# A two-layer graph network: indexed stores without addition, and the residual added by VectorE from PSUM

## The chip, the cores and the metric

The kernel runs on one core of a Trainium2 chip. The metric is the device time of one execution in microseconds; the median of several runs is given. PE is TensorE (matrix products), DVE is VectorE, ACT is ScalarE, POOL is GpSimd, SP is the engine that only issues DMAs here. Each engine takes its instructions in a fixed order, and an instruction that waits holds up all behind it on its engine.

## The reference

There are 16 graphs of 1024 nodes with 64 features each, and a weighted adjacency matrix of 1024 x 1024 for each. Cut to what matters:

```python
# layer 0
h = maximum(layernorm(x), 0)
deg = clip(sum(adj, axis=2, keepdims=True), 1.0, None)
x = x + matmul(adj / deg, h)

# layer 1
h = maximum(layernorm(x), 0)
adj_d = dilate(adj, mask)     # self loops set; of a node with over 10 neighbours every
                              # skip-th one is removed, in both directions
agg = weighted sum of the 0.25, 0.5 and 0.75 quantiles (weights 0.25, 0.5, 0.25) of
      h over the neighbours in adj_d, feature by feature
y = relu((h + agg) @ W1 + b1) @ W2 + b2
x = x + y * mask
```

`W1` is 64 x 128 and `W2` is 128 x 64. The last line is the one that the change is about: each node's result is its residual `x` after layer 0 plus its masked sum.

## The kernel before, in words

**A planner writes the order.** The kernel is built from Python generators ("streams"). Each stream yields the engine that it needs next and a time before which it shouldn't start. `Plan` (from L231) keeps an estimated clock for each engine and for every tile the time at which it is ready, always runs the stream that can start first, and records the instructions. Their order on every engine is therefore settled when the program is built, from estimated costs. Since every instruction passes through one helper, most of them carry line 225 in the profile; one goes by tile names. Two margins occur in what follows: a stream asks to start `SLACK` = 2 us, or `LOOSE` = 7 us, after the estimated time at which its input is ready. `room(name, n)` is the estimated time at which the oldest of n buffers is free again. Any indirect DMA on POOL is estimated at 1.27 us (L292).

**Layer 0**, graph by graph (streams `loads`, `beginnings`, `signs`, `listing`, `transposes`, `products`, `channels`, `endings`). SP loads the adjacency matrix in eight tiles `at` of 128 x 1024, with five buffers. ACT takes their signs, DVE makes of each row a list of neighbours (32 candidates, `rec`), PE transposes them and multiplies by the normalised features. The result x1 (the residual) is written into a tile `row` (L565), which for each node holds, in this order: 64 normalised features and two index columns (width W = 66), the record of 34 columns (the list, the node's number and its mask) and the residual of 64. `channels` (L700) normalises x1, stores the residual of the whole graph to `out` (L708), and the features to a table `tab` in DRAM (L709). `endings` (L714) gives every node a place by the length of its list, and POOL stores the features and the record (100 columns) to that place of a sorted table `srt` with eight indirect DMAs for each graph (L775). Four graphs share one `srt`; there are four such groups.

**Layer 1** works on 128 nodes of like list length at once. `group` (L1016) loads the records of a sorted table and makes ten `Job`s, of one to six tiles of 128 nodes, with lists of 15 neighbours down to 1. A job (L808) loads the nodes' own rows (`S`, L821) by SP, gathers the neighbours' rows from `tab` with one indirect DMA on POOL for each tile and neighbour (`places`), and sorts them on DVE with a network of minimum and maximum operations. The quantiles are products with weights (`prod`). `long_lists` (L1134) does the same for the longest lists, 20 to 88 neighbours (`lplaces`), with one tile of 128 nodes for each.

**The layers' end** is `layers` (L964). For up to four tiles at a time: PE sums and transposes the terms into `pt`, ACT evacuates it to `ot`, PE multiplies by `W1` into PSUM, ACT applies bias and relu (`hid`), PE multiplies by `W2` and adds the bias `b2`: for each tile there is one product of 128 x 64, and one of a row of ones with `b2_sb`. ACT then multiplies by the mask into `y` (L1003 to L1007), and POOL adds `y` to the nodes' rows of `out`, with an indirect DMA that adds to what stands there (L1012). The four buffers of `y` are freed by the store.

```python
for i, t in enumerate(ts):
    nc.tensor.matmul(pv[:, i, :], hid[:, i * P:(i + 1) * P], w2_sb, start=True, stop=False)
    nc.tensor.matmul(pv[:, i, :], ones_f[:1, :], b2_sb, start=False, stop=True)
yield "ACT", lambda: at(py) + SLACK
for i, t in enumerate(ts):
    nc.scalar.activation(y[:, t, :], pv[:, i, :], AF.Copy, scale=self.mask[:, t:t + 1])
```

Stores to one table have no order among themselves, since they go to different rows; `scatter` (L786) declares that, and puts a small memset of the tile `turn` between two stores to the same table that follow one another directly. All this is `list_path` (L364). A second path, `dense_path`, is only taken when a list overflows, and doesn't run on these inputs.

Of the kernel before, what the change touches and what calls it, by code (L numbers as in the profile page):

```python
# [9 lines left out]
F32 = mybir.dt.float32  # L10
# [4 lines left out]
AF = mybir.ActivationFunctionType  # L15
OP = mybir.AluOpType
AX = mybir.AxisListType

P = 128
# [8 lines left out]
GB = 4  # L28
# [184 lines left out]
SLACK = 2.0  # L213
LOOSE = 7.0
# [16 lines left out]
class Plan:  # L231
# [132 lines left out]
def list_path(ctx, tc, x, adj, nodemask, w1, b1, w2, b2, out, go):  # L364
    nc = tc.nc
    B, N, C = x.shape
    H = w1.shape[1]
    CO = w2.shape[1]
    NT = N // P
    HALF = 512  # L370
    BPH = HALF // P
    NG = B // GB
    TS = N + 1
    W = C + 2
    PW = W // 2
    REC = 8 * NSEG + 2
    R0 = W
    X1 = RW = R0 + REC
    NTAU = N // SUB
    NF = NG + NG + len(LONG)  # L380

# [58 lines left out]
    nc.sync.dma_start(w2_sb, w2)  # L440
    b1_sb = consts.tile([H, 1], F32, name="b1_sb")
    nc.sync.dma_start(b1_sb, b1.rearrange("(h o) -> h o", o=1))
    b2_sb = consts.tile([1, CO], F32, name="b2_sb")
    nc.sync.dma_start(b2_sb, b2.rearrange("(o c) -> o c", o=1))
    taus = consts.tile([P, len(QUANTILES)], F32, name="taus")
    for k, (tau, wt) in enumerate(QUANTILES):
        nc.vector.memset(taus[:, k:k + 1], tau)
# [24 lines left out]
    scatters = []  # L472
    sorts = [[] for _ in range(NG)]
    plan = Plan(nc)
    nc = plan.nc
# [79 lines left out]
    def beginnings(pool, now):  # L555

        for b, st in enumerate(batch):
            now[0] = b
            yield "DVE", lambda: max(known(st, "xt", "mrow"), room("h0", 3), room("row", 4))
            mrow_f = new(tiny, [NT, P], F32, "mrow_f", 2)  # L560
            nc.vector.tensor_copy(mrow_f, st["mrow"])

            h0 = new(pool, [P, NT, C + 1], F32, "h0", 3, users=2)
            nc.vector.memset(h0[:, :, C:], 1.0)
            row = st["row"] = new(pool, [P, NT, X1 + C], F32, "row", 4, users=1)  # L565
            nc.vector.memset(row[:, :, C:W], -1.0)
            yield from normed(h0[:, :, :C], st["xt"])
            st["h0"] = h0
            yield "PE", lambda: max(at(mrow_f), room("ps_small", 3))
            pm = new(ps_s, [P, HALF], F32, "ps_small", 3, users=1)  # L570
            nc.tensor.transpose(pm[:, :NT], mrow_f, ident[:NT, :NT])
            yield "ACT", lambda: at(pm)
            nc.scalar.copy(row[:, :, RW - 1], pm[:, :NT])
            nc.scalar.copy(row[:, :, RW - 2], row_f)
            free(pm)
# [79 lines left out]
    def products(pool, now):  # L655


        for b, st in enumerate(batch):
            now[0] = b
            for hf in range(2):  # L660
                yield "PE", lambda: INF if st["copied"][hf] < 2 * BPH else max(
                    at(st["att"][hf]), known(st, "h0"), room("ps_small", 3)
                )
                po = new(ps_s, [P, HALF], F32, "ps_small", 3, users=1)
                for q in range(NT):
                    if q and q % 2 == 0:
# [12 lines left out]
                pb = new(ps_s, [P, HALF], F32, "ps_small", 3, users=1)  # L679
                sums = pb[:, :BPH * (C + 1)].rearrange("p (k c) -> p k c", c=C + 1)  # L680
                for k in range(BPH):
                    nc.tensor.transpose(
                        sums[:, k, :], msg[:, k * P:(k + 1) * P], ident[:C + 1, :C + 1]
                    )
                yield "DVE", lambda: at(pb) + SLACK
                x1 = st["row"][:, hf * BPH:(hf + 1) * BPH, X1:]
                deg = new(tiny, [P, BPH], F32, "deg", 2)
                nc.vector.tensor_scalar(deg, sums[:, :, C], 1.0, None, op0=OP.max)
                nc.vector.reciprocal(deg, deg)
                nc.vector.tensor_tensor(  # L690
                    x1, sums[:, :, :C], deg.unsqueeze(2).to_broadcast([P, BPH, C]), OP.mult
                )
                nc.vector.tensor_tensor(
                    x1, x1, st["xt"][:, hf * BPH:(hf + 1) * BPH, :], OP.add
                )
                free(pb)
                st["residual"] += 1
            free(st["xt"])

    def channels(pool, now):  # L700

        for b, st in enumerate(batch):
            now[0] = b
            row = lambda: st["row"]
            yield "DVE", lambda: known(st, "row") if st["residual"] == 2 else INF
            yield from normed(row()[:, :, :C], row()[:, :, X1:])

            nc.sync.dma_start(out[b].rearrange("(t p) c -> p t c", p=P), row()[:, :, X1:])  # L708
            nc.sync.dma_start(  # L709
                tab[b * TS:b * TS + N, :].rearrange("(t p) w -> p t w", p=P), row()[:, :, :W]  # L710
            )
            st["normed"] = True

    def endings(pool, now):  # L714

        first = lambda rank: rank - 3000
        for b, st in enumerate(batch):
# [54 lines left out]
            nc.vector.scalar_tensor_tensor(to, low, float(1 - GB), pos, op0=OP.mult, op1=OP.add)  # L772
            for t in range(NT):
                yield "POOL", lambda: max(at(to), at(row)) + LOOSE if "normed" in st else INF, first
                scatter(srt[g], row[:, t, :RW], to[:, t:t + 1], sorts[g])  # L775
            free(row)
            progress["batches"] = b + 1

# [4 lines left out]
            in_offset=bass.IndirectOffsetOnAxis(ap=idx, axis=0),  # L783
        )

    def scatter(dst, src, idx, others, op=OP.bypass):  # L786
        if plan.last is others:
            nc.gpsimd.memset(turn, 0.0)
        ins = nc.gpsimd.indirect_dma_start(
            out=dst, out_offset=bass.IndirectOffsetOnAxis(ap=idx, axis=0),  # L790
            in_=src, in_offset=None, compute_op=op,
        )

        for other in others:
            tc.declare_no_dep(ins.ins, other, reason="rows of their own")
        others.append(ins.ins)
        plan.last = others

    class Job:
# [8 lines left out]
        def run(self):  # L808
# [9 lines left out]
            progress["ahead"] += T * (n - 1)  # L818
            if short:
                mine = self.S  # L820
                self.S = new(pool, [P, T, W], F32, "S", 4, users=1)  # L821
                nc.sync.dma_start(self.S, mine)
            for t in range(T):
                for k in range(n - 1):
                    if t or k:
# [138 lines left out]
        def layers(self, terms, sources):  # L964

            T, R = self.T, terms[0][0].shape[1]
            yield "PE", lambda: max(at(*sources) + LOOSE, room("y", 4), room("pt", 2))
            y = new(mlp, [P, T, CO], F32, "y", 4, users=1)
            for t0 in range(0, T, 4):
                ts = range(t0, min(t0 + 4, T))  # L970
                M = len(ts) * P
# [23 lines left out]
                yield "PE", lambda: max(at(hid) + SLACK, room("ps_small", 3))  # L995
                py = new(ps_s, [P, HALF], F32, "ps_small", 3, users=1)
                pv = py[:, :len(ts) * CO].rearrange("p (t c) -> p t c", c=CO)
                for i, t in enumerate(ts):
                    nc.tensor.matmul(
                        pv[:, i, :], hid[:, i * P:(i + 1) * P], w2_sb, start=True, stop=False  # L1000
                    )
                    nc.tensor.matmul(pv[:, i, :], ones_f[:1, :], b2_sb, start=False, stop=True)
                yield "ACT", lambda: at(py) + SLACK  # L1003
                for i, t in enumerate(ts):
                    nc.scalar.activation(
                        y[:, t, :], pv[:, i, :], AF.Copy, scale=self.mask[:, t:t + 1]
                    )  # L1007
                free(py)
            for t in range(T):
                yield "POOL", lambda: at(y) + LOOSE  # L1010
                rows = out_rows[:min(self.g + 1, NG) * GB * N, :]
                scatter(rows, y[:, t, :], self.nodes_i[:, t:t + 1], scatters, OP.add)  # L1012
            free(y)
            progress["jobs"][self.g] += 1

    def group(g):  # L1016
# [107 lines left out]
        for i, ts in enumerate(classes):  # L1124
            n, T = CAPS[ts[0]] + 1, len(ts)
            sl = slice(ts[0], ts[-1] + 1)
            job = Job(
                gat, n, T, keys[:, sl, :n - 1], idx[:, sl, :], node[:, sl], mask[:, sl],
                nodes_i[:, sl], table, tiles[:, sl, :W], g,
            )  # L1130
            plan.add(job.run(), 100 * g + i)
        progress["groups"] = g + 1
# [393 lines left out]
```

## Time and profile before

| | |
|---|---|
| median of 3 runs | 1586.0 us (1583.88 to 1586.02) |
| the profiled execution's own time | 1823.34 us, of which the profile's span is 1821.4 |
| indirect DMAs of POOL | 660 gathers of rows from `tab`, 128 stores to `srt`, 128 stores to `out` |
| `y` on ACT | 128 instructions, 0.313 us each in the median |
| bias products on PE | 256 passes |
| moved by DMA | 124.89 MB, 69 GB/s over the span |
| mean granted clock of TensorE | 0.653 of full speed |

The profiled execution is longer than the timed ones, since recording costs time. Durations and differences below are therefore read inside the profile and compared with its own length. In the page, a group of instructions is named by what it writes and reads (`out<-in`), with its count, busy time and mean duration, and after the second bar the time that its engine stood idle just before it, with what ended that idle time. A releaser called "issue" is none that the profile shows. PE makes two passes for one product in fp32, and each is counted.

### The profile page before, as it was taken

How to read it: one execution, taken by the hardware profiler on the slowest of the kernel's cores; microseconds unless marked ns; L12 is line 12 of the kernel's file. 1: busy time of each engine (PE TensorE's matmuls, PEld its weight loads, DVE VectorE, ACT ScalarE, POOL GpSimd, SP SyncE). 2: the span in 40 equal slices, each digit the busy share in tenths (PEclk: the TensorE clock that was granted, in tenths of full speed). 3: DMA queues.
4: the chain of work that ended last, by engine and by line, in shares of the span. 5: the costliest groups of instructions: out<-in, count | busy, mean ns of one | idle time of the engine just before them, and what ended most of it. 6: DMA issues, size and time to landing. Idle time of an engine off the chain costs nothing. (4 is left out here: it accounts for less than half of the span.)

```text
span 1821.4 us, 15210 instructions
## 1 busy us (share of the span) xinstructions
PE 825.6 (45%) x3336; PEld 533.0 (29%) x3336; DVE 1240.1 (68%) x4046; ACT 609.3 (33%) x1874; POOL 1050.8 (58%) x1144
## 2 busy tenths in 40 slices
PE   5767822365686572563685000110031366253364
PEld 3333411233444341232354000100021245242343
DVE  7865858475788486678642889339497678896622
ACT  8877653245655464444442000000010111010011
POOL 0112263636467655555758766567656788575757
PEclk8978855675798675775885555555555567555656
DMA  5544741233444353353222211101111112111112
GB/s 170 163 133 122 199 125 31 48 101 81 121 134 112 58 134 91 90 138 73 56 48 49 43 43 34 23 17 22 28 24 28 18 26 20 23 30 23 24 18 17
DMA packets 147941, 124.89 MB, mean 69 GB/s; under 512 B 117715, under 2 KB 117843, under 8 KB 147843
## 3 DMA queue, kind: packets, MB, share of 16 engines
q1 hardware_dynamic: 102818, 86.58, 16.8%
q0 software_dynamic: 45024, 37.28, 12.2%
q14 instruction: 71, 0.57, 0.1%
q8 instruction: 28, 0.46, 0.1%
HBM read 104.51 MB, written 19.28 MB: 68 GB/s over the span
## 5 line engine op out<-in xcount | busy, mean ns | idle before, releaser
L225 POOL DMA_INDIRECT places<-tab,idx x496 | 495.0, 998 | 165.1 <-issue 140.2
L225 PE MATMUL pt<-ident,prod 128*128 128x128 f32 (+1 forms) x736 | 161.8, 384 | 569.4 <-DVE prod L225 294.5
L225 POOL DMA_INDIRECT out_dram<-y,nodes_i x124 | 208.0, 1678 | 186.8 <-ACT y L225 127.4
L225 PEld LDWEIGHTS pt<-ident,prod 128*128 128x128 f32 (+1 forms) x736 | 134.2, 267 | 605.3 <-issue 389.7
L225 POOL DMA_INDIRECT srt<-row,to x128 | 129.4, 1011 | 259.0 <-ACT row L225 223.5
L225 PE MATMUL pt<-ident,at 128*128 128x128 f32 x1024 | 190.0, 334 | 179.6 <-ACT att L225 72.1
L225 PE MATMUL ps_small<-att,h 128*65 128x512 f32 x512 | 259.0, 652 | 17.7 <-ACT h L225 10.3
L225 PEld LDWEIGHTS pt<-ident,at 128*128 128x128 f32 x1024 | 143.5, 171 | 236.5 <-ACT att L225 97.7
L225 POOL DMA_INDIRECT lplaces<-tab,lidx x163 | 171.0, 1049 | 49.7 <-issue 49.1
L225 ACT COPY att<-pt 128x512 f32<-128x512 f32 x256 | 142.9, 583 | 155.7 <-remote 84.2
L225 DVE MAX8 rec<-sg 128x8 f16<-128x256 f16 x512 | 180.1, 414 | 9.5 <-remote 5.2
L225 ACT ACTIVATE wu<-wu 128x39 f32<-128x39 f32 (+9 forms) x40 | 9.4, 234 | 431.7 <-DVE wu L225 168.8
L225 ACT ACTIVATE sg<-at 128x1024 f16<-128x1024 f32 x128 | 134.9, 1055 | 31.7 <-DMA at<-in_adj_dram 15.3
L225 DVE TENSOR_TENSOR sg<-sg,keyed 128x1024 f16<-128x1024 f16 x128 | 87.4, 683 | 65.5 <-issue 33.4
L225 PEld LDWEIGHTS ps_small<-att,h 128*65 128x65 f32 x512 | 75.4, 153 | 149.4 <-issue 126.5
L225 ACT COPY ot<-pt 128x128 f32<-128x128 f32 (+3 forms) x56 | 22.4, 400 | 246.7 <-remote 128.2
L225 PE MATMUL ps_small<-ot,w_sb 128*128 128x128 f32 (+3 forms) x112 | 55.9, 593 | 104.7 <-ACT ot L225 72.6
L225 PE MATMUL ps_small<-w_sb,hid 128*128 128x64 f32 x256 | 72.5, 376 | 52.6 <-ACT hid L225 25.1
L225 DVE TENSOR_TENSOR other<-places,other 128x64 f32<-128x64 f32 (+6 forms) x204 | 69.5, 341 | 35.6 <-remote 16.3
L225 PEld LDWEIGHTS ps_small<-w_sb,hid 128*128 128x128 f32 x256 | 53.6, 258 | 80.5 <-ACT hid L225 40.3
L225 DVE TENSOR_TENSOR rem<-places,recs 128x30 f32<-128x30 f32 (+9 forms) x40 | 7.3, 182 | 101.7 <-DMA places<-tab,idx 90.0
L225 POOL MEMSET turn<- 128x1 f32 x204 | 76.2, 373 | 0.1
(206 smaller groups left out, 1712.2 us busy)
## 6 DMA issues: line engine op xcount, KB each, us to landing
at<-in_adj_dram SPq DMA_DIRECT2D x128, 512.0 KB
places<-tab,idx POOLq DMA_INDIRECT x496
tab<-row SPq DMA_DIRECT2D x16, 264.0 KB
xt<-in_x_dram SPq DMA_DIRECT2D x16, 256.0 KB
out_dram<-row SPq DMA_DIRECT2D x16, 256.0 KB
lplaces<-tab,lidx POOLq DMA_INDIRECT x163
recs<-srt SPq DMA_DIRECT2D x4, 544.0 KB
srt<-row,to POOLq DMA_INDIRECT x128
```

What stands on the lines that cost most here:

```text
L225: ins = getattr(self._engine, op)(*args, **kwargs)
```

## The change

The residual no longer goes to `out` early. It becomes part of the rows that POOL sorts (164 columns in place of 100), and is added in the last step of layer 1.

- The tile `row` is laid out anew: features and index columns, residual, record. The whole row is stored to `srt`.
- The 16 stores of the residual to `out` by SP go.
- `S` is loaded with 64 columns in place of 66. A job with short lists keeps a reference to the residual's columns, and loads them into the tile `y` at the head of `layers`, by SP. A long list has them in its `S` already.
- `b2_sb` holds the bias four times, and one product of the row of ones with up to 256 columns takes the place of up to four; it comes first in the group.
- The last sum is formed by VectorE: PSUM times mask plus residual, in place into `y`. It is planned `LOOSE` after the product, where ACT's was planned `SLACK` after it. `y` has five buffers, not four.
- The indirect store to `out` is a plain one, and names all rows of `out`.

```diff
-    R0 = W
-    X1 = RW = R0 + REC
+    X1 = W
+    R0 = X1 + C
+    RW = R0 + REC
...
-    b2_sb = consts.tile([1, CO], F32, name="b2_sb")
-    nc.sync.dma_start(b2_sb, b2.rearrange("(o c) -> o c", o=1))
+    b2_sb = consts.tile([1, 4 * CO], F32, name="b2_sb")
+    for k in range(4):
+        nc.sync.dma_start(b2_sb[:, k * CO:(k + 1) * CO], b2.rearrange("(o c) -> o c", o=1))
...
-            yield from normed(row()[:, :, :C], row()[:, :, X1:])
-
-            nc.sync.dma_start(out[b].rearrange("(t p) c -> p t c", p=P), row()[:, :, X1:])
+            yield from normed(row()[:, :, :C], row()[:, :, X1:R0])
...
-                scatter(srt[g], row[:, t, :RW], to[:, t:t + 1], sorts[g])
+                scatter(srt[g], row[:, t, :], to[:, t:t + 1], sorts[g])
...
-                self.S = new(pool, [P, T, W], F32, "S", 4, users=1)
-                nc.sync.dma_start(self.S, mine)
+                self.S = new(pool, [P, T, C], F32, "S", 4, users=1)
+                nc.sync.dma_start(self.S, mine[:, :, :C])
+                self.residual = mine[:, :, X1:R0]
...
-            yield "PE", lambda: max(at(*sources) + LOOSE, room("y", 4), room("pt", 2))
-            y = new(mlp, [P, T, CO], F32, "y", 4, users=1)
+            yield "PE", lambda: max(at(*sources) + LOOSE, room("y", 5), room("pt", 2))
+            y = new(mlp, [P, T, CO], F32, "y", 5, users=1)
+            x1 = y
+            if self.short:
+                nc.sync.dma_start(x1, self.residual)
+            else:
+                x1 = self.S[:, :, X1:R0]
...
+                nc.tensor.matmul(
+                    py[:, :len(ts) * CO], ones_f[:1, :], b2_sb[:, :len(ts) * CO],
+                    start=True, stop=False,
+                )
                 for i, t in enumerate(ts):
                     nc.tensor.matmul(
-                        pv[:, i, :], hid[:, i * P:(i + 1) * P], w2_sb, start=True, stop=False
+                        pv[:, i, :], hid[:, i * P:(i + 1) * P], w2_sb, start=False,
+                        stop=(i == len(ts) - 1),
                     )
-                    nc.tensor.matmul(pv[:, i, :], ones_f[:1, :], b2_sb, start=False, stop=True)
-                yield "ACT", lambda: at(py) + SLACK
+                yield "DVE", lambda: at(py) + LOOSE
                 for i, t in enumerate(ts):
-                    nc.scalar.activation(
-                        y[:, t, :], pv[:, i, :], AF.Copy, scale=self.mask[:, t:t + 1]
+                    nc.vector.scalar_tensor_tensor(
+                        y[:, t, :], pv[:, i, :], self.mask[:, t:t + 1], x1[:, t, :],
+                        op0=OP.mult, op1=OP.add,
                     )
                 free(py)
+
             for t in range(T):
                 yield "POOL", lambda: at(y) + LOOSE
-                rows = out_rows[:min(self.g + 1, NG) * GB * N, :]
-                scatter(rows, y[:, t, :], self.nodes_i[:, t:t + 1], scatters, OP.add)
+                scatter(out_rows, y[:, t, :], self.nodes_i[:, t:t + 1], scatters)
```

Since the planner's estimates and waits change, it writes another order for all engines, from the first microseconds on.

More of the change, by code (lines that the diff above doesn't have):

```diff
@@ L564, in beginnings @@
             nc.vector.memset(h0[:, :, C:], 1.0)
-            row = st["row"] = new(pool, [P, NT, X1 + C], F32, "row", 4, users=1)
+            row = st["row"] = new(pool, [P, NT, RW], F32, "row", 4, users=1)
             nc.vector.memset(row[:, :, C:W], -1.0)
@@ L685, in products @@
                 yield "DVE", lambda: at(pb) + SLACK
-                x1 = st["row"][:, hf * BPH:(hf + 1) * BPH, X1:]
+                x1 = st["row"][:, hf * BPH:(hf + 1) * BPH, X1:R0]
                 deg = new(tiny, [P, BPH], F32, "deg", 2)
@@ L784, in gather, with scatter @@
         )
-    def scatter(dst, src, idx, others, op=OP.bypass):
+    def scatter(dst, src, idx, others):
         if plan.last is others:
@@ L790, in scatter @@
             out=dst, out_offset=bass.IndirectOffsetOnAxis(ap=idx, axis=0),
-            in_=src, in_offset=None, compute_op=op,
+            in_=src, in_offset=None,
         )
@@ L1128, in group @@
                 gat, n, T, keys[:, sl, :n - 1], idx[:, sl, :], node[:, sl], mask[:, sl],
-                nodes_i[:, sl], table, tiles[:, sl, :W], g,
+                nodes_i[:, sl], table, tiles[:, sl, :R0], g,
             )
```

## The prediction

> **What bounds the kernel now.** I read the page first: busy time by engine and the forty slices.
>
> ```profile
> span 1821.4 us, 15210 instructions
> ...
> PE 825.6 (45%) x3336; PEld 533.0 (29%) x3336; DVE 1240.1 (68%) x4046; ACT 609.3 (33%) x1874; POOL 1050.8 (58%) x1144
> ...
> PE   5767822365686572563685000110031366253364
> ...
> DVE  7865858475788486678642889339497678896622
> ...
> POOL 0112263636467655555758766567656788575757
> ```
>
> No engine is full over the span, and there are two stages. In the first 22 slices PE, ACT and DVE work together (layer 0); later PE and ACT are nearly empty and only DVE and POOL stay busy. The tile view of `srt` puts the last sorting store at 988.4 us, so I cut at 990 and asked for busy time by window:
>
> ```profile
> core 0: us, PE busy (x) PEld busy (x) DVE busy (x) ACT busy (x) POOL busy (x), PEclk, DMA share, GB/s
> 0.00:990.00 990.00, 590.65 (x2345) 348.17 (x2346) 674.76 (x2252) 545.58 (x1670) 488.47 (x600) 0.73 0.40 104
> ```
>
> Then the groups of POOL alone from 990 to 1822 (count, busy, mean; after the second bar the idle time ahead of them and what ended it):
>
> ```profile
> L225 POOL DMA_INDIRECT places<-tab,idx x243 | 247.0, 1016 | 75.2 <-issue 67.1 <-DMA places<-tab,idx 4.6 <-DMA tab<-drop,didx 1.4
> L225 POOL DMA_INDIRECT lplaces<-tab,lidx x163 | 171.0, 1049 | 49.7 <-issue 49.1 <-DMA lplaces<-tab,lidx 0.6
> L225 POOL DMA_INDIRECT out_dram<-y,nodes_i x73 | 125.2, 1715 | 111.2 <-ACT y L225 77.2 <-ACT prod L225 21.1 <-issue 12.0
> ...
> L225 POOL DMA_INDIRECT out_dram<-y,lnodes_i x4 | 6.5, 1626 | 5.3 <-ACT wu L225 4.4 <-issue 0.9
> ```
>
> The "issue" gaps of 0.3 us stand between any two indirect DMAs and belong to them. Gathers so cost 247.0 + 75.2 + 171.0 + 49.7 = 543 us. The 77 result stores take about 1.89 us from start to start (below), 145 us. Waits for `y` and what is booked with them are 77.2 + 21.1 + 4.4 = 103 us, the rest (adjacency gathers and their waits) about 28. Together 819 of 832 us: the second stage is POOL's queue, with 103 us of holes in which it stands at a store whose sum isn't there.
>
> The timeline of POOL shows what one store costs, accumulating first, plain second:
>
> ```profile
> 1758.43 1.58 POOL L225 DMA_INDIRECT out_dram<-y,nodes_i  x1 [0.19 <-issue]
> 1759.44 0.68 POOL L225 MEMSET turn<- 128x1 f32 x1
> 1760.32 1.57 POOL L225 DMA_INDIRECT out_dram<-y,nodes_i  x1 [0.19 <-issue]
> ```
>
> ```profile
> 246.64 0.98 POOL L225 DMA_INDIRECT srt<-row,to  x1 [0.19 <-ACT row L225]
> 247.62 0.11 POOL L225 MEMSET turn<- 128x1 f32 x1
> 247.93 0.97 POOL L225 DMA_INDIRECT srt<-row,to  x1 [0.19 <-issue]
> ```
>
> Start to start, 1760.32 - 1758.43 = 1.89 us against 247.93 - 246.64 = 1.29. At the end of the program seventeen stores follow one another at this rate, to a last start at 1812.35, and nothing comes after them. In the first stage POOL waits instead: 205.9 of its idle us before 926 end on `row` from ACT.
>
> **What the Trainium skill says.** "DMA: Bandwidth & Descriptors", SWDGE vs HWDGE vs iDMA: an accumulating DMA can be issued by GpSimd only, and GpSimd cores compute the descriptors of indirect DMAs. The trace agrees: all 128 are POOL's, at a median of 1.58 us against 0.97 for a plain store; the page has no price for the accumulation. "Perfetto Trace Analysis", DMA Instruction — SWDGE (GPSIMD): the shown duration ends with the last descriptor written, not with the data. So 1.58 and 0.97 are POOL's own time, and it is POOL that the change relieves. "SBUF — State Buffer", Who interferes with whom: a VectorE instruction with at most one SBUF tensor outside the two-port modes doesn't contend with GpSimd; the new sum reads PSUM and one SBUF tensor. No run here shows that instruction.
>
> **The change part by part.** Sums are of the profiled execution: its time is 1823.34 us, the span 1821.4 and 1.9 around it. The median of the runs is 1586.0, 0.870 of it; which rows recording lengthens isn't visible, so I scale differences by 0.870.
>
> *Plain stores.* 1.89 - 1.28 (between 1.27 and 1.29 for `srt`) = 0.61 us each, 128 x 0.61 = 78 us of POOL. The order of the two programs says where: after the last sorting store there are 77 result stores and 406 gathers now, 83 and 399 after. Second stage: stores 145 to 83 x 1.28 = 106, -39; gathers 543 to 399 x 543/406 = 534, -9. Together -48 us. The first stage holds 45 stores (51 now) and 7 gathers more. It saves POOL 51 x 1.89 - 45 x 1.28 - 7 x 1.34 = 29 us, but waits for rows there take more than that: 0. Bounds for a store that is plain but goes to `out`: 0.97 (as `srt`), and 1.58 if the cost is of the destination and not of the addition. I take 0.97, since gathers from `tab` and stores to `srt` differ by only 0.03 us.
>
> *The last sum on VectorE.* 128 ACT instructions of 0.313 us go (40 us, ACT 33% busy, so nothing). 128 DVE instructions are added, 128 x 64 with a PSUM source and two tensors. Nearest row: TENSOR_TENSOR on 128x64, 0.22 to 0.23 us; at 128x256 a PSUM source costs the same as an SBUF one (`row<-ps_small,deg` 0.424, `row<-row,xt` 0.430). So 128 x 0.23 = 29 us, 83 x 0.23 = 19 in the second stage and 10 in the first. DVE has room in both (565 busy of 832, 675 of 990), but feeds POOL's waits: I put half of the 19 on the path, +10; bounds 0 and 19.
>
> *The wait on DVE.* Each of 56 groups of sums (four tiles or fewer) now makes DVE's queue wait for PE's product; behind it are the comparisons of other lists, and behind those the gathers' buffers. ACT idles 38.6 + 78.3 = 117 us before `y` (before and after the cut, nearly all for `ps_small`). But the planner puts the sum 7 us after its estimate of the product, not 2, and most of these waits are short (longest 5.1 us but for three or four). Taken: 0, bounds 0 and 117.
>
> *Residual.* SP gets 40 loads of 256-byte rows and loses 16 stores of 256 KB, about as many rows. They start at the head of the layers, before transposes, two products and two evacuations: some 10 us ahead of the sum in the timeline (1783.1 to 1793.0 for one of the last lists), hidden. 35 of them wait for an older store from the same of five buffers; behind them on SP stand loads of `at` (first stage) and `S`. ACT waited only 15.3 us in all for `at`, so some cover is there: 0, bounds 0 and 15. The sorting rows grow from 400 to 656 bytes and 128 x 128 x 256 B = 4.2 MB move over from the removed store of `out`: DMA is 0.40 busy in the first stage, nothing. Three more loads of the bias at the start: a fraction of a us, ahead of the first `at`: 0 to 1.
>
> *One bias product.* Per group of four, eight bias passes at 0.31 us start to start become two of 256 columns (0.58, as `ps_small<-ot,w_sb` 128x256): -1.3 us in the chain to `y`. PE is 0.28 busy in the second stage, so only the latency counts, at most a few us; 0.
>
> Sum: -48 + 10 = -38 us of the profile, x 0.870 = -33: 1553. A few us of shorter chains to `y` at the last jobs: **1550**.
>
> **Rivals.**
> - *Larger gain.* Every indirect DMA costs 1.27 in the planner; accumulating stores cost 1.58 and hold back all that is planned behind them. With plain ones plan and chip agree, and half of the 103 us of holes close: -38 - 52 = -90, x 0.870: 1508. For it: in the hole ending at 1756.5, ACT had taken `wu` of a later list first, which waited 20.95 us for its gathers, with `ot` behind. Against: planned sums are 5 us later.
> - *Little or nothing.* DVE and POOL take turns (DVE waits 107 us for gathers in the second stage), so only half of the 48 arrives, and all 19 of DVE: -5, 1582. The case of stores that stay dear falls here too (+10 - 9 = about 0).
> - *Slower.* DVE stands at the sums. If half of the 117 us is on the path with all 29 of work: 58 + 29 - 48 = +39, x 0.870: 1620. It decides from 48 - 29 = 19 us of standing. Place: sums placed between the comparisons of a long list, where each late product stops all sorting. Against: the later placing.
>
> **How the numbers follow.** Forecast 0.47, larger gain 0.17, little or nothing 0.14 (0.10 of it still faster), slower 0.22. Measurement tells about 0.2% (3 us) from no change. So faster 0.74, same 0.04, slower 0.22. The likeliest case alone spans 1530 to 1572. The range goes from 1500 (a little beyond the middle of the larger gain) to 1605 (below the middle of the slower case), which leaves out about 0.18.
>
> **What would show it.** Right: result stores at 0.97 us and 1.28 start to start; sums of 0.23 us on DVE; last sorting store still near 988; the second stage some 40 us shorter. Wrong: stores still near 1.58; DVE idle before `y` above 20 us in all; POOL's waits for `y` above 103 us; the last sorting store past 1000, which would point to SP's waits.

## The result and the profile after

The changed kernel takes 1569.51 us (median of 4 runs, 1568.55 to 1573.65), against 1585.32 (1583.88 to 1586.02) for the kernel before: a ratio of 0.9905, with a 95% interval of 0.9889 to 0.9921. It is 15.8 us faster, where 35 had been predicted: a gain that is clear of the noise, and less than half of the forecast.

The page of the changed kernel, in the lines that were shown of the kernel before:

```profile
span 1571.9 us, 14933 instructions
...
PE 744.4 (47%) x3192; PEld 465.3 (30%) x3192; DVE 1260.4 (80%) x4174; ACT 578.5 (37%) x1746; POOL 989.3 (63%) x1149
...
PE   5787776365756754855880001200021367124355
...
DVE  6767899997997699999556897659779889878962
...
POOL 0222238665578767568676666587777678566775
```

The span is 250 us shorter than that of the profile before, which can't be the change. The first experiment therefore recorded the kernel before again, and got 1582.3 us:

```profile
span 1582.3 us, 15210 instructions
...
PE 790.2 (50%) x3336; PEld 512.1 (32%) x3336; DVE 1237.6 (78%) x4046; ACT 607.7 (38%) x1874; POOL 1060.2 (67%) x1144
```

The busy times of DVE, ACT and POOL are within 1% of those of the profile on record (DVE 1240.1, ACT 609.3, POOL 1050.8), and PE's is 4% lower (825.6 there); it is the gaps that are smaller. The profile before was taken under conditions in which the whole kernel takes some 15% longer (the last section returns to this). What was said of it ahead of the prediction, that recording costs time, does not hold: recorded again, the kernel took 1584.19 us, as long as its other runs. All that follows compares with the second recording, where nothing else is said.

Busy time by window, cut at the last sorting store; the columns are the window, its length, and the busy time and instructions of PE, weight loads, DVE, ACT and POOL, then clock, DMA share and GB/s. The kernel before, recorded again:

```profile
0.00:826.90 826.90, 569.10 (x2380) 337.83 (x2380) 673.08 (x2252) 546.62 (x1681) 494.10 (x599) 0.80 0.49 124
826.90:1583.00 756.10, 221.09 (x956) 174.28 (x956) 564.55 (x1794) 61.05 (x194) 566.11 (x546) 0.56 0.21 29
```

The changed kernel:

```profile
0.00:826.20 826.20, 553.21 (x2307) 315.87 (x2307) 682.14 (x2311) 533.54 (x1619) 466.18 (x596) 0.80 0.46 127
826.20:1573.00 746.80, 191.19 (x886) 149.43 (x886) 578.27 (x1863) 44.98 (x127) 523.17 (x554) 0.56 0.16 32
```

The first stage is as long as it was, and the second 9 us shorter, though POOL has 43 us less to do in it. Where the rest went is in the groups of POOL in the second stage. Before (recorded again):

```profile
L225 POOL DMA_INDIRECT out_dram<-y,nodes_i x73 | 119.8, 1642 | 39.0 <-ACT y L225 18.2 <-issue 12.9 <-ACT prod L225 7.3
L225 POOL MEMSET turn<- 128x1 f32 x55 | 38.8, 706 | 0.0
```

Changed:

```profile
L225 POOL DMA_INDIRECT out_dram<-y,nodes_i x79 | 83.9, 1062 | 60.0 <-DVE y L225 41.3 <-issue 9.6 <-DVE lrem L225 5.4
L225 POOL MEMSET turn<- 128x1 f32 x64 | 7.6, 118 | 0.0
```

A store costs POOL 0.97 us in the median, and follows another after 1.27: as predicted. But POOL waits 41.3 us for `y` where it waited 18.2. Why `y` comes late stands in the waits of DVE in the second stage (total, times, longest). Changed:

```profile
DVE y L225 <- PE ps_small L225: 74.1, 16, 9.4
DVE lrem L225 <- DMA lplaces<-tab,lidx: 21.7, 1, 21.7
DVE rem L225 <- DMA places<-tab,idx: 14.0, 1, 14.0
```

Before (recorded again):

```profile
DVE rem L225 <- DMA places<-tab,idx: 63.1, 8, 20.7
DVE lrem L225 <- DMA lplaces<-tab,lidx: 38.6, 2, 36.2
```

DVE stands 74.1 us at its new sums (80.9 in the whole kernel), and 66 us less for gathers. In the kernel before, the last sums were ACT's, and ACT stood 92.1 us for the same products, in 46 places. The sums themselves are one group in the page:

```profile
L225 DVE SCALAR_TENSOR_TENSOR y<-ps_small,recs,y 128x64 f32<-128x64 f32 x124 | 28.0, 276 | 81.0 <-PE ps_small L225 80.9
```

One lasts 266 to 286 ns from start to end, so none was held up once begun. Two that follow one another overlap: 124 of them keep DVE busy for 28.0 us, 0.23 us each. One place where DVE stands, in the timeline of all engines (start, duration, and in brackets the idle time before it):

```profile
1404.89 0.55 DVE L225 SCALAR_TENSOR_TENSOR places<-gone,places 128x384 f32<-128x384 f32 x1
...
1407.17 0.37 ACT L225 COPY ot<-pt 128x256 f32<-128x256 f32 x1 [1.54 <-PE pt L225]
...
1407.59 1.07 PE L225 MATMUL ps_small<-ot,w_sb 128*128 128x256 f32 x2 [0.46 <-ACT ot L225]
...
1408.70 0.47 ACT L225 ACTIVATE hid<-ps_small,b_sb 128x256 f32<-128x256 f32 x1 [1.16 <-PE ps_small L225]
...
1409.23 0.66 PE L225 MATMUL ps_small<-w_sb,hid 128*128 128x64 f32 x4 [0.15 <-ACT hid L225]
1409.92 0.47 DVE L225 SCALAR_TENSOR_TENSOR y<-ps_small,recs,y 128x64 f32<-128x64 f32 x2 [4.48 <-PE ps_small L225]
1410.32 0.89 DVE L225 TENSOR_TENSOR long_other<-lplaces 128x128 f32<-128x128 f32 x2
1410.48 0.98 POOL L225 DMA_INDIRECT out_dram<-y,nodes_i  x1 [8.05 <-DVE y L225]
```

DVE ends its work at 1405.44 and reaches the sum before the first of its four links (`ot`, product, `hid`, product) has begun. It stands 4.48 us, with the comparisons of a long list (`long_other`) behind it, whose inputs don't depend on this sum; POOL stands 8.05 us at the store.

### The profile page after: what moved, and what is told of

Same layout as the page of the kernel before. It is cut to its first block, busy times and chain, and to the rows that moved or that the text cites. A ratio compares the mean times of both kernels' runs of the same rounds, so it can differ in the third digit from the quotient of the medians.

```text
span 1571.9 us, 14933 instructions
## 1 busy us (share of the span) xinstructions
PE 744.4 (47%) x3192; PEld 465.3 (30%) x3192; DVE 1260.4 (80%) x4174; ACT 578.5 (37%) x1746; POOL 989.3 (63%) x1149
## 5 line engine op out<-in xcount | busy, mean ns | idle before, releaser
L225 POOL DMA_INDIRECT places<-tab,idx x496 | 507.4, 1023 | 159.9 <-issue 146.1
L225 PE MATMUL pt<-ident,prod 128*128 128x128 f32 (+1 forms) x736 | 168.0, 395 | 627.5 <-DVE prod L225 586.7
L225 PE MATMUL pt<-ident,at 128*128 128x128 f32 x1024 | 167.3, 308 | 80.7 <-ACT att L225 68.9
L225 POOL DMA_INDIRECT out_dram<-y,nodes_i x124 | 130.6, 1053 | 99.2 <-DVE y L225 53.6
L225 PEld LDWEIGHTS pt<-ident,at 128*128 128x128 f32 x1024 | 129.4, 157 | 126.2 <-ACT att L225 93.7
L225 DVE SCALAR_TENSOR_TENSOR y<-ps_small,recs,y 128x64 f32<-128x64 f32 x124 | 28.0, 276 | 81.0 <-PE ps_small L225 80.9
L225 DVE TENSOR_TENSOR places<-places,other 128x64 f32<-128x64 f32 (+2 forms) x208 | 62.4, 309 | 4.9
L225 DVE TENSOR_TENSOR long_other<-lplaces 128x512 f32<-128x512 f32 (+5 forms) x124 | 63.9, 553 | 0.4
L225 DVE TENSOR_TENSOR lplaces<-long_other 128x512 f32<-128x512 f32 (+7 forms) x116 | 61.4, 567 | 0.1
L225 DVE TENSOR_TENSOR places<-other,places 128x128 f32<-128x128 f32 (+5 forms) x160 | 54.9, 343 | 3.5
```

What stands on the lines that cost most here:

```text
L225: ins = getattr(self._engine, op)(*args, **kwargs)
```

## The experiments

The first theory is that standing: DVE, the engine with most to do, waits in order for a product that the planner thought ready. The rivals: the work of the sums itself (DVE's busy time rises from 1237.6 to 1260.4 us); the late loads of the residual by SP; and the order. Since every edit of an estimate gives another order on all engines, a difference can be the chance of the order alone. All gains below are against the kernel before, run beside it on the same chip. The "addition of the residual" is left out where said, so that `out` holds only the masked sum.

### The kernel before again

No edit.

> The kernel before, unchanged, profiled once more. If recording itself lengthens it, the profiled execution takes about 1820 us again with the first stage near 990 us. If the profile of before was one odd execution, it takes about 1586, like the profiled execution of the changed kernel, which was no longer than its timed ones.

1584.19 us, span 1582.3 (above).

### Plain stores alone

```diff
-                scatter(rows, y[:, t, :], self.nodes_i[:, t:t + 1], scatters, OP.add)
+                scatter(rows, y[:, t, :], self.nodes_i[:, t:t + 1], scatters)
```

The kernel before with this one edit; the addition of the residual is left out. The planner costs both stores alike, so the order on every engine is that of the kernel before.

> The kernel before with plain result stores and nothing else, in the same order on every engine (the residual, which went to the output earlier, is overwritten, so the addition of the residual is left out). Theory POOL: the stores are the whole of the gain and the rest of the change gives a part of it back, so 1545 to 1560. Theory order: the new order made the gain, and cheap stores alone give 1580 to 1586. Theory that the second stage is bound by DVE: about 1575, the stores at the end of the program alone (17 x 0.61 = 10 us).

1548.51 us (1547.62 to 1552.29), ratio 0.9754 [0.9736, 0.9771]: -39.6 us, free of any change of order, and within what was expected if POOL's stores are what costs. The prediction had -48 x 0.870 = -42. The two stages of the recorded execution (span 1549.6):

```profile
0.00:820.00 820.00, 565.97 (x2380) 336.89 (x2380) 673.36 (x2252) 546.68 (x1681) 460.27 (x598) 0.80 0.46 125
820.00:1550.00 730.00, 220.80 (x956) 174.58 (x956) 564.65 (x1794) 60.24 (x193) 520.41 (x546) 0.56 0.16 30
```

POOL has 46 us less to do in the second stage, and the stage is 26 us shorter; the first, where the prediction put no gain, is 7 us shorter. In the second stage DVE waits 90.0 us for the gathers of `rem` and `lrem`, where it waited 101.7, so a part of POOL's shorter queue reaches DVE; POOL itself stands 15 us longer at the result stores (53.6 against 39.0).

### The last sums on ScalarE in the changed kernel

```diff
-                yield "DVE", lambda: at(py) + LOOSE
+                yield "ACT", lambda: at(py) + SLACK
                 for i, t in enumerate(ts):
-                    nc.vector.scalar_tensor_tensor(
-                        y[:, t, :], pv[:, i, :], self.mask[:, t:t + 1], x1[:, t, :],
-                        op0=OP.mult, op1=OP.add,
+                    nc.scalar.activation(
+                        y[:, t, :], pv[:, i, :], AF.Copy, scale=self.mask[:, t:t + 1]
                     )
```

The late load of the residual goes too, and its addition is left out.

> The changed kernel with the last sums on ACT again, planned 2 us after the product, and without loading or adding the residual (that addition is left out). Theory that DVE stands at the sums: 28 us of work and up to 81 us of idle time ahead of them go, 1535 to 1550. Theory that DVE's part costs little: 1560 to 1570. Theory order: anything between 1560 and 1595, with no relation to DVE's idle time.

1524.38 us (1521.72 to 1526.84), 0.9599 [0.9583, 0.9616], below all that was expected. Without VectorE's sums and the late loads the change is worth 61 to 64 us, not 16. The 45 us between this kernel and the changed one are of the sums, the loads and the other order together.

### The same sums on VectorE, waiting for nothing

```diff
+                yield "DVE", lambda: at(py) + LOOSE
+                scr = new(mlp, [P, 2, CO], F32, "scr", 1)
+                for i, t in enumerate(ts):
+                    nc.vector.scalar_tensor_tensor(
+                        scr[:, i % 2, :], ones_f[:, :CO], self.mask[:, t:t + 1], ones_f[:, CO:],
+                        op0=OP.mult, op1=OP.add,
+                    )
```

Put into the kernel of the last experiment: 128 sums of the same size, on constants.

> The version with the sums on ACT (1524.4, addition of the residual left out), with 128 VectorE instructions of the same size added at the places of the sums, which read constants and wait for no product. If DVE's work is what costs, most of the 45 us between that version and the changed kernel come back: 1550 to 1570. If the standing at the sums is what costs, only the 35 us of work come in as far as DVE is the bound: 1530 to 1545.

1530.67 us (1529.55 to 1531.88), 0.9632 [0.9612, 0.9653], as expected if the standing is what costs. Against the last experiment DVE is busy for 24.1 us more (1260.7 against 1236.6), its waits for the gathers of `rem` and `lrem` fall from 100.2 to 73.3 us over the whole kernel, and the end comes 6 us later. So most of the work seems to fall into time in which DVE would have waited. But the order is another one here too (the last sorting store moves from 810.3 to 869.7 us), and 6 us is less than an order can be worth, as will be seen. The other 39 of the 45 belong to the wait, the loads or the order.

### The sums planned earlier and later

```diff
-                yield "DVE", lambda: at(py) + LOOSE
+                yield "DVE", lambda: at(py) + SLACK
```

The changed kernel with the sums 2 us after the estimated product, not 7; then likewise with 14.0 and 21.0. Nothing is left out.

> The changed kernel with the sums planned 2 us after the product in place of 7. Theory that DVE stands at the sums: its idle time ahead of y grows from 81 us by up to 5 us for each of 56 groups, and the time by 10 to 60 us, 1580 to 1630. Theory that DVE's part costs little: 1565 to 1575.

> The changed kernel with the sums planned 14 us after the product in place of 7. If the standing costs, DVE's idle time ahead of y falls well below 81 us and the time to 1540 to 1560. If the work or the residual's loads cost, 1565 to 1575.

> The changed kernel with sums planned 21 us after the product. DVE's idle time ahead of y (143, 81 and 21 us for 2, 7 and 14) falls to near 0. If standing alone counts, 1505 to 1520; if later sums hold back the stores and buffers by then, 1525 to 1545.

2 us: 1599.95 (1595.4 to 1609.18), 1.0069 [1.0046, 1.0092]. 14 us: 1524.74 (1520.56 to 1526.25), 0.959 [0.9567, 0.9613]. 21 us: 1540.44 (1538.46 to 1543.54), 0.9701 [0.9668, 0.9733]. The wait of DVE for the product, over the whole kernel, at 2 us:

```profile
DVE y L225 <- PE ps_small L225: 143.3, 25, 14.4
```

At 14 us:

```profile
DVE y L225 <- PE ps_small L225: 21.3, 6, 5.0
```

The two stages at 14 us:

```profile
0.00:828.20 828.20, 540.91 (x2308) 307.28 (x2308) 689.97 (x2334) 532.86 (x1622) 467.95 (x597) 0.81 0.47 127
828.20:1523.00 694.80, 190.79 (x884) 149.01 (x884) 570.04 (x1841) 43.90 (x124) 518.61 (x551) 0.57 0.18 35
```

Five microseconds in the plan make the difference between slower than before and faster; seven more the other way bring 45 us, with all work and all loads of the residual kept. At 2, 7 and 14 us the recorded first stages last 830.1, 826.2 and 828.2 us, the second ones 777, 746 and 695: the whole difference lies in the stage in which DVE stands. As far as the order lets one tell, the loads cost nothing, since this kernel has them and is as fast as the one with neither loads nor sums on DVE (1524.38). At 21 us the standing did not fall to near 0, as had been expected, but to 28.6 us.

### The same kernels in another order

```diff
-            time, after = 0.05, 2.2 + math.prod(out.shape) * 4 / 165e3
+            time, after = 0.05, 2.2 + math.prod(out.shape) * 4 / 160e3
```

A slightly lower DMA rate in the planner's estimates changes no instruction, only the order. It was put into the changed kernel, into plain stores alone (the addition of the residual left out), and into the one with 14 us.

> The changed kernel with one estimate of the planner altered by 3% (the bytes that a DMA moves in a us), so that the same instructions stand in a slightly other order. It measures what order alone does: if the differences so far are of the edits, within 8 us of 1569.5; if they are chance of the order, anywhere from 1530 to 1600.

> The same altered estimate in the kernel before with plain stores (1548.5, addition of the residual left out). If the single bias product made the 17 us between it and the kernel with that product, this stays within 8 us of 1548.5; if order alone can do that, it lies near 1530 or as far on the other side.

> The same altered estimate in the changed kernel with sums planned 14 us late (1524.7). If the later place is what counts, DVE stands about 20 us ahead of y again and the time is within 8 us of 1525; if that order was lucky, 1540 and more.

Changed kernel: 1574.55 (1572.07 to 1585.82), 0.9932 [0.9903, 0.9961], against 1569.51. Plain stores: 1538.98 (1530.0 to 1545.43), 0.9698 [0.9642, 0.9754], against 1548.51. With 14 us: 1552.93 (1550.26 to 1555.95), 0.979 [0.9756, 0.9824], against 1524.74. So an order is worth 5, 10 and 28 us by chance alone. By the mark set ahead (1540 and more), the first order of the kernel with 14 us was a lucky one. With the same estimate on both sides, 14 us in place of 7 bring 45 us in one pair of orders and 22 (1574.55 to 1552.93) in the other. One pair of differently ordered kernels shows nothing below the worth of an order; the pattern of several has to.

Six kernels form the sums on VectorE from PSUM with one instruction each, and differ only in the plan:

| kernel | DVE's wait for the product, us | time, us |
|---|---|---|
| 14 us | 21.3 | 1524.74 |
| 14 us, other order | 27.0 | 1552.93 |
| 21 us | 28.6 | 1540.44 |
| changed kernel (7 us) | 80.9 | 1569.51 |
| changed kernel, other order | 100.4 | 1574.55 |
| 2 us | 143.3 | 1599.95 |

A straight line through these rises by 0.51 us for each us of standing (standard error 0.08) and meets no standing at 1526 us. None of the six lies more than 13 us off it, which is less than an order can be worth. The kernel with the same work and no wait, which isn't among them, has 1530.67. For the changed kernel the line gives 0.51 x 80.9 = 42 us. The three with over 80 us of standing are all slower than the three with under 30, by 42 us in the mean and 17 at the closest. That speaks for the standing, and the kernels without a wait speak with it. But the margin in the plan was changed to move the standing, and can act in other ways too; it isn't the proof that one edit in a kept order would be.

### Mask on ScalarE, one addition for four tiles on VectorE

```diff
-                yield "DVE", lambda: at(py) + LOOSE
+                yield "ACT", lambda: at(py) + SLACK
...
-                    nc.vector.scalar_tensor_tensor(
-                        y[:, t, :], pv[:, i, :], self.mask[:, t:t + 1], x1[:, t, :],
-                        op0=OP.mult, op1=OP.add,
+                    nc.scalar.activation(
+                        pv[:, i, :], pv[:, i, :], AF.Copy, scale=self.mask[:, t:t + 1]
                     )
+                yield "DVE", lambda: at(py) + 14.0
+                sl = slice(t0, t0 + len(ts))
+                nc.vector.tensor_tensor(y[:, sl, :], pv, x1[:, sl, :], OP.add)
```

> A complete version: ACT multiplies by the mask in PSUM, VectorE adds the residual of up to four tiles in one instruction, planned 14 us after ACT's. VectorE's work falls from 35 to some 20 us and its standing below 81 us. If both count, 1530 to 1550 and below both kernels; if the later sums delay the stores, about 1570.

1555.73 (1553.28 to 1558.64), 0.9791 [0.9768, 0.9813], where 1530 to 1550 was expected. Less work on DVE and as little standing (22.3 us, now for ACT), but no better than the plain late plan, and 18 us above the line of the six kernels. A fifth link in the chain to `y`, and again another order, are in this number; why it is no better is not shown.

### One bias product in the kernel with plain stores

```diff
...
+                nc.tensor.matmul(
+                    py[:, :len(ts) * CO], ones_f[:1, :], b2_sb[:, :len(ts) * CO],
+                    start=True, stop=False,
+                )
                 for i, t in enumerate(ts):
                     nc.tensor.matmul(
-                        pv[:, i, :], hid[:, i * P:(i + 1) * P], w2_sb, start=True, stop=False
+                        pv[:, i, :], hid[:, i * P:(i + 1) * P], w2_sb, start=False,
+                        stop=(i == len(ts) - 1),
                     )
-                    nc.tensor.matmul(pv[:, i, :], ones_f[:1, :], b2_sb, start=False, stop=True)
```

The addition of the residual is left out.

> The kernel before with plain stores (1548.5, addition of the residual left out) and the single bias product. If the bias product carries the 24 us between that kernel and the one with the sums on ACT: 1525 to 1535. If not (removed stores of the residual, or the order): 1543 to 1550.

1531.23 (1527.55 to 1532.66), 0.9628 [0.9605, 0.9651]: 17 us below plain stores alone, but in another order, and 8 below plain stores in the other order. What the bias product is worth can't be told from what the order is.

### Four attempts to keep the order, on a slower chip

To part wait, work and order, the planner was given the old instruction at the old place (`plan.note` costs an instruction without issuing it), and another was issued.

```diff
...
-                    nc.vector.scalar_tensor_tensor(
-                        y[:, t, :], pv[:, i, :], self.mask[:, t:t + 1], x1[:, t, :],
-                        op0=OP.mult, op1=OP.add,
+                    tc.nc.scalar.activation(
+                        y[:, t, :], pv[:, i, :], AF.Copy, scale=self.mask[:, t:t + 1]
                     )
+                    tc.nc.vector.scalar_tensor_tensor(
+                        scr[:, i % 2, :], ones_f[:, :CO], self.mask[:, t:t + 1], ones_f[:, CO:],
+                        op0=OP.mult, op1=OP.add,
+                    )
+                    plan.note(
+                        "DVE", "scalar_tensor_tensor",
+                        (y[:, t, :], pv[:, i, :], self.mask[:, t:t + 1], x1[:, t, :]), {},
+                    )
```

The second attempt drops the sums on constants as well; the third and fourth work on plain stores alone: the single bias product, and the early stores of the residual left out. The addition of the residual is left out in all four. In the traces POOL's order is kept in each, and that of the other engines in the fourth. In the first three some instructions of PE and ACT stand elsewhere, at most 84 of about 3100 on PE and 79 of about 1700 on ACT.

> The changed kernel in its own order on every queue: ScalarE forms mask times product at the places where VectorE formed the sums, and VectorE does, at those same places, 128 sums of the same size on constants, which wait for nothing. Left out: the addition of the residual to the output (it is still loaded). If the changed kernel loses its time by VectorE standing at its sums, the standing (some 80 us) goes and the work stays: 1525 to 1545. If the time is that of the order in which the work was planned, which is unchanged here: 1560 to 1575.

> As the run above, but VectorE does nothing at those places. Against it this prices the work of the 128 sums alone in one order (128 x 0.276 = 35 us of VectorE time): standing theory 5 to 20 us below the run above, so 1515 to 1535; if VectorE's work fell into its idle time altogether, no difference; order theory 1555 to 1575.

> The kernel before with plain stores (the residual's addition left out), and the single bias product put in without any change to the planned order of the work. If the single product shortens TensorE's chain by what the rows say (1.3 us for each of 40 groups), and that chain is what the end waits for: up to 50 us below plain stores alone, and the 17 us of the earlier run would come back, 1525 to 1535. If the earlier 17 us were those of another order: 1543 to 1553, as plain stores alone.

> The kernel before with plain stores, in its order, and without the early stores of the residual rows to the output (which is then left out of it). If these stores cost SP or the DMA queues anything that the end waits for: 1535 to 1545. If they are hidden: 1545 to 1553, as plain stores alone.

These ran on a chip on which the kernel before takes 1823.67 us (1815.85 to 1831.22). No wait: 1860.89, 1.0212 [1.0178, 1.0246]. No wait and no work: 1855.99, 1.0187 [1.0157, 1.0218]. Single bias product: 1836.42, 1.007 [1.0043, 1.0097]. No early stores: 1851.4, 1.0176 [1.0133, 1.0219]. The first and the third were run once more, and met the same chip:

> The same kernel as in e13, because e13 met a chip on which the kernel before itself takes 1824 us (as in its profile on record), against 1584 to 1589 us on the others. On a chip of the latter kind: 1525 to 1545 if the changed kernel (1570) loses its time by VectorE standing at the sums, 1560 to 1575 if by the order. On a chip of the first kind: about 1860 again, which tells the two apart in neither case.

> The same kernel as in e15, for the same reason. On a chip where the kernel before takes 1584 to 1589 us: 1525 to 1535 if the single bias product is worth the 17 us of e7, 1543 to 1553 if those were the order's.

1884.35, 1.0184 [1.0154, 1.0215], and 1851.92, 1.0006 [0.9984, 1.0027], with the kernel before at 1850.13.

The expectations of these six were worked out for a chip on which the kernel before takes 1584 to 1589 us, so they decide nothing between the theories; the one value named for this chip, about 1860 for the first kernel run again, was missed by 24 us. What the runs show: with POOL's order kept, 128 sums that wait for nothing cost about 5 us or nothing (the intervals overlap), which agrees with the 6 above. And on this chip none of the kernels with plain stores was faster than the kernel before.

The fourth shows where POOL's relief went there, since its order is that of the kernel before; the profile on record, taken under like conditions (1823.34 us), stands beside it. POOL's busy time is lower by 82 us (968.9 against 1050.8). But in the second stage POOL stands 145.3 us at the stores of short lists, where it stood 111.2; the stage is 3 us shorter (829.8 against 833.0), and the first is 19 us longer (1007.7 against 988.4). Most of the time that POOL saved became waiting at the stores. Why the first stage is longer is open: it also differs between two runs of one kernel (1031.2 and 1040.3 for the first of the four).

The changed kernel itself, and plain stores alone, were not run on this chip. Wait against order in the changed kernel's own order, and the price of the bias product in a kept order on the other chips, stay untested.

## Why the prediction was right about the stores and wrong about the wait

| step | predicted | measured |
|---|---|---|
| plain stores | -48 us of the profile, -42 of the time, all in the second stage | -39.6 of the time, in the same order; of 33 us recorded, 26 in the second stage |
| last sorting store | unmoved | 826.9 to 826.2 |
| sums on DVE | 0.23 us each, 29 in all | 0.23 each of DVE's time; 23 to 24 more of its busy time in all |
| sums on DVE, on the path | +10 (0 to 19), +9 of the time | +6 in another order (and 5 or nothing on the slower chip) |
| wait of DVE | 0 (0 to 117) | 80.9 us of standing; by the pattern of the plans some 39 to 42 on the path |
| rows, early stores, bias product, order | 0, less a few | -24 where the sums stay on ACT, not parted |

The last row is the difference between the sums left on ScalarE (1524.38) and plain stores alone (1548.51). The times add up, 1588 - 39.6 - 24 + 6 + 39 = 1569, because each is the difference between one kernel and the next. Only the first was measured in one order; the others carry what an order is worth.

**The step that failed** is "The wait on DVE", in the words "Taken: 0, bounds 0 and 117". Two reasons were given for 0. The first was that most of ACT's waits before `y` were short. They were read from an engine that is busy for 61 of 756 us in the second stage, where a wait holds up little; DVE is busy for 578 of 746, and holds up all that is queued behind. (The 117 leave out the stretch between the two windows; the lines of the profile on record give 124.) The second was that a margin of 7 us, not 2, would cover most of the waits. They became fewer, 18 in place of 46, but longer, 4.5 us in place of 2.0 in the mean, and 80.9 us in all; a margin of 14 left 21.3. The mark that the prediction set for being wrong, over 20 us of idle DVE before `y`, was passed fourfold. That DVE stands is measured. What the standing costs was not measured in a kept order: the line of the six plans gives 42 us, and the kernel with the same work and no wait lies 39 us lower.

**Of the slower rival** the mechanism happened and the sum was wrong. Its 19 us are what must lie on the path; as it counts half of the standing, that is 38 us of standing. With the 80.9 us that came, it would have had 40 + 29 - 48 = +21 us, and the kernel is still faster. Two of its terms differ: the work, 29 us there and 6 between the two kernels above, and the 24 us of the last row, which were not in its sum. That half of the standing counts is what it assumed and what the line says. One reason fits the traces: DVE was already idle in the second stage, for gathers, and standing at a sum gives a gather time to land. The waits for `rem` and `lrem` fell from 101.7 to 35.7 us as the 74.1 came; over the whole kernel they are 35.9 us in the changed kernel, and 78.9 where the sums are planned 14 us after the product. No run moves one and holds the other.

**The profile underneath.** The 103 us of holes on `y`, on which the larger gain rested, are 18.2 + 7.3 us in the second recording. That rival had little to close. The other waits were read from the same profile. Scaling by 0.870 came close for the stores, -42 to -39.6, but its reason, recording, did not hold, and part of the agreement is luck: the prediction put all of it into the second stage, where 26 of 33 us were found; and under the conditions of the profile from which the 48 were read, none of the kernels with plain stores that were run was faster.

**Plain stores.** The rows of POOL said what they cost, and the median of 0.97 us for a plain store to `out` rules out that the destination made the price. With nothing else changed, POOL's busy time fell from 1060.2 to 980.7, which is 0.62 for each of 128 stores where the rows had said 0.61, and half of it reached the end (39.6 of 79.5).

A version that beats both kernels is the changed one with the sums planned 14 us after the product: 0.959 [0.9567, 0.9613] in an order that turned out lucky, and still 0.979 [0.9756, 0.9824] in the other.

## What to carry to other kernels

Before moving the evacuation of a late product to another engine, take the old engine's waits ahead of it and ask what they would cost on the new one: a wait that holds up little on a nearly idle engine can hold up much on the engine that feeds the rest. If the place in the queue is set by an estimate, try the margin itself, over a wide range, before judging the move. And where an edit makes a planner write another order, measure what an order alone is worth (here 5 to 28 us), and trust only differences that are larger or that keep the order.

## What was not expected of the hardware

Two chips, or two conditions, differ by 15% for one program: 1588 to 1589 us in the median on the three chips of the first twelve runs, 1824 and 1850 on the one of the last six, and 1823.34 in the profile on record. DVE's instructions last equally long (1240.1 us of busy time against 1237.6), and the gaps between them make the difference: the first stage lasts 988.4 us against 826.9. They open even between DVE instructions that follow one another in one computation. In the profile on record:

```profile
378.50 0.18 DVE L225 TENSOR_TENSOR rem<-places,recs 128x28 f32<-128x28 f32 x1
380.69 0.17 DVE L225 TENSOR_TENSOR gone<-rem 128x14 f32<-128x14 f32 x1 [2.01 <-remote]
382.09 0.17 DVE L225 SCALAR_TENSOR_TENSOR ok<-keys,gone 128x14 f32<-128x14 f32 x1 [1.23 <-DVE gone L225]
```

The same three instructions in the second recording:

```profile
318.80 0.18 DVE L225 TENSOR_TENSOR rem<-places,recs 128x28 f32<-128x28 f32 x1
319.01 0.20 DVE L225 TENSOR_TENSOR gone<-rem 128x14 f32<-128x14 f32 x1
319.25 0.17 DVE L225 SCALAR_TENSOR_TENSOR ok<-keys,gone 128x14 f32<-128x14 f32 x1
```

What holds the engines there isn't shown by any run. In all seven profiles of this kind about half of the semaphore records are missing (13110 in the profile on record, 24207 in the second recording), so the length of a wait can be read there, but what ended it less surely. It matters for the reading: a profile whose span is far from the timed runs should be recorded again before its waits are counted.
